# A Mamba layer on Trainium2: one bank of PSUM moved from the states of the scan to the small products beside it

## The chip, the cores and the metric

The kernel runs on one core of one Trainium2 chip. The core has a matmul engine (TensorE, "PE" in the profile, with its weight loads as "PEld"), a vector engine (VectorE, DVE), an activation engine (ScalarE, ACT), a general one (GpSimd, POOL) and a queue from which most DMAs are issued (SyncE, SP). Each engine works through its own instructions in order, and waits on semaphores for the others. Matmuls write into PSUM, which VectorE and ScalarE read and write too; in this kernel it is handed out in eight banks of 512 fp32 values a partition. The metric is the device time of one execution in microseconds, lower is better; times are medians of several executions.

## The reference

A network of four layers over an image of 2 x 256 x 48 x 48 in fp32: a Mamba layer (layer 0), linear attention with a convolution and a feed-forward (layer 1), attention and a graph-gated mixture (layer 2), sigmoid attention and a routed mixture (layer 3). The change lies in layer 0, whose core is a selective scan, run over the 2304 pixels once forward and once backward:

```python
def _selective_scan(u, delta, A, Bm, Cm, D):
    h0 = jnp.zeros((Bsz, d, A.shape[1]), u.dtype)
    def step(h, xs):
        d_t, B_t, C_t, u_t = xs
        dA = jnp.exp(d_t[..., None] * A)
        h = dA * h + (d_t * u_t)[..., None] * B_t[:, None, :]
        y = jnp.einsum('bdn,bn->bd', h, C_t)
        return (h, y)
    ...
    return ys.transpose(1, 0, 2) + u * D

def _mamba_branch(xi, z, conv_w, conv_b, xproj_w, dtproj_w, dtproj_b, A_log, D):
    ...                                     # depthwise convolution of 4 taps: xc
    xs = jax.nn.silu(xc + conv_b[None, :, None]).transpose(0, 2, 1)
    proj = xs @ xproj_w.T
    dt = jax.nn.softplus(proj[..., :DT_RANK] @ dtproj_w.T + dtproj_b)
    Bm = proj[..., DT_RANK:DT_RANK + D_STATE]
    Cm = proj[..., DT_RANK + D_STATE:]
    y = _selective_scan(xs, dt, -jnp.exp(A_log), Bm, Cm, D)
    return y * jax.nn.silu(z)

h = _layernorm(seq, ln_g, ln_b) + pos
xz = h @ in_proj_w.T
xi, z = (xz[..., :d_inner], xz[..., d_inner:])
y = (y_f + y_b) @ out_proj_w.T
out = seq + y
```

There are 512 inner channels (`DB` = 4 blocks of 128 partitions) and 16 states for each (`NS`). The scan is a recurrence along the pixels, one for each channel and state.

## The kernel before

Everything is fp32. Layer 0 cuts the 2304 pixels of each of the two images into six pieces of 384 (`W`). A piece in one direction of one image is a *scan*: 2 images x 2 directions x 6 pieces = 24 scans, in the list `order`. Each call of `scan` (L499) works through 4 blocks x 16 states = 64 states, and carries the last column of each over to the next piece in `state`.

For one state the engines pass a tile on:

- ScalarE writes the decay exp(dt * A) into a PSUM tile `hs` (L544). These tiles come from the pool `psh`, tag "hs": five banks before the change.
- VectorE runs the recurrence over it (L550 forward, L553 backward), with `db`, the product of dtu and B, which GpSimd makes for four states at a time (L527). For five of every eight states the result goes back into the same bank `hs`, for three into an SBUF tile `ho`.
- The result times C is the product `hc` (L558): made by VectorE from `hs`, by GpSimd from `ho`. Each of the two has four SBUF buffers.
- ScalarE copies the last column into `state` (L560), except in the last piece of a direction.
- TensorE adds `hc` to the output of its block by a matmul with the identity (L512), into `yp`. Those two banks (pool `psy`) stay as they are; L533 and L537 start them.

So a bank `hs` is held from the exponential until the product and the state copy have read it, or, where the result goes to `ho`, until the recurrence has.

Beside each scan runs other work, in small steps that are written into the loop after every second state (L568 to L572): `prepare` for the next scan, in 15 steps (convolution L311 and its copy L315, SiLU L321, the projection L327, the matmuls for dt L341 with L344 and L345, softplus L347 to L357, dtu on GpSimd L359); for the first ten scans `project_in` for a later piece, in 12 steps (layer norm L221 to L240, matmuls L247 and copies L252); after a backward scan `project_out`, in 2 steps (L368 and the sum L373), followed by the statistics of `piece_stats` (L138); and in the later scans the weights and contexts of layers 1 and 2 (`head_products`, `contexts`: pg, pu, pk, pc and others, L392 to L494). Each of these products takes one PSUM tile from the pool `ps`, tag "mm", through `hold` or directly: one bank before the change. It is free again when ScalarE or VectorE has read the product.

`hold` has a second case. Before the first scan (`scanning` is false) it takes its tiles from `psh`:

```python
    def hold():

        pool, tag = (ps, "mm") if scanning else (psh, "hs")
        return pool.tile([P, 512], F32, tag=tag, name="mm")[:, :W]
```

The order of instructions on each engine is made when the program is built, by the framework's ordering of what the source says, with the buffers that are free; it is not the order of the source line by line. ScalarE switches between tables for exponential, SiLU, logarithm and square root (ACT_TABLE_LOAD in the profile).

Of the kernel before, what the change touches and what calls it, by code (L numbers as in the profile page):

```python
# [24 lines left out]
PSUM = bass.MemoryType.PSUM  # L25
# [148 lines left out]
def layer0(ctx, E):  # L174
# [9 lines left out]
    nc, tc, p = E.nc, E.tc, E.p  # L184
# [5 lines left out]
    dr = ctx.enter_context(tc.tile_pool(name="l0d", bufs=2, space=DRAM))  # L190
    wp = ctx.enter_context(tc.tile_pool(name="l0w", bufs=2))
    up = ctx.enter_context(tc.tile_pool(name="l0u", bufs=1))
    psh = ctx.enter_context(tc.tile_pool(name="l0ps_h", bufs=5, space=PSUM))
    ps = ctx.enter_context(tc.tile_pool(name="l0ps_s", bufs=1, space=PSUM))
    psy = ctx.enter_context(tc.tile_pool(name="l0ps_y", bufs=1, space=PSUM))

    load_x(E, 0, 0)
# [1829 lines left out]
@with_exitstack  # L2027
def hybrid_kernel(ctx: ExitStack, tc: tile.TileContext, p: dict):
    E = Env(ctx, tc, p)
    layer0(E)  # L2030
    with tc.tile_pool(name="norm", bufs=1) as pool:

        E.xn = pool.tile([P, 2, T], F32, name="xn")
        with ExitStack() as kept:
            edges = Edges(kept, E)
            layer1(E, edges)
            with tc.tile_pool(name="gedge", bufs=1) as wp:
                edges.sort_rest(E, wp)
                layer2_attn(E)
            layer2_ffn(E, edges)  # L2040
        layer3(E)
    store_out(E)
# [73 lines left out]
```

## Time and profile before

| | |
|---|---|
| median of 3 runs | 5328.02 us (5325.92 to 5332.41) |
| profiled execution | 5324.93 us, span 5323.1 us |
| TensorE clock granted, mean | 0.963 |
| first and last recurrence of layer 0 | 101.9 and 2448.9 us |
| one scan, from its first recurrence to the next one's | 89 to 108 us, the last 80 us |
| one recurrence L550/L553 | 0.93 to 1.01 us |
| one product L558: VectorE, GpSimd | 0.54, 1.03 us |
| one exponential L544, one state copy L560 | 0.58, 0.15 to 0.19 us |
| one db L527 (four states) | 3.44 us |
| one ACT_TABLE_LOAD | 1.28 us, 65 of them before L544 |

The page gives for each engine its busy time over the whole program, and its share in 40 slices of 133 us. A row of instructions has the line, the engine, the tiles written and read, busy time and mean duration, then the idle time of the engine just before them and who ended it. A matmul of fp32 stands as two records, so four products of a convolution are "x8". A row of waits gives the waiting instruction, the one that ended the wait, the total, the count and the longest. In the timeline a line is the start, the duration, the engine, the line of the code and the tiles, with the idle time in brackets.

### The profile page before, as it was taken

Reading aid. Unit: us, or ns where it says so; the run is one execution under the profiler, and the core shown is the slowest. Engines: PE = TensorE matmul, PEld = TensorE weight load, DVE = VectorE, ACT = ScalarE, POOL = GpSimd, SP = SyncE. Lnnn points to the kernel's source line nnn. Section 1 sums busy time; section 2 is a strip of 40 time slices with the busy share of each in tenths; the row PEclk is TensorE's granted clock in tenths of the full one; section 3 lists DMA queues with packets and bytes.
Section 4 is the critical chain, followed back from the end, with each engine's and each line's share of the span. In section 5 each row is a group of like instructions: output and inputs, shape, how many; then the busy total and the mean of one; then the engine's idle time right before and its main releaser. Section 6 shows DMA issues by size and latency. Waiting matters only on the chain. (4 is left out here: it accounts for less than half of the span.)

```text
span 5323.1 us, 47473 instructions
## 1 busy us (share of the span) xinstructions
PE 4760.4 (89%) x15282; PEld 2640.7 (50%) x15282; DVE 3489.3 (66%) x5378; ACT 2385.4 (45%) x4985; POOL 2415.8 (45%) x1320
## 2 busy tenths in 40 slices
PE   7888888888888888888999989999999999999997
PEld 3444444444444444444555555556655555555675
DVE  4999898989898888899999344546734411212343
ACT  5767767765667667762223223432133322222221
POOL 2888887788888878884000000028712100000321
PEclk8999999999999999999999999999999999999998
DMA  4454454444444344443110000111121100000422
GB/s 154 169 174 170 164 178 165 168 177 166 163 165 161 137 157 161 149 152 118 38 48 28 3 16 0 35 32 31 19 96 48 48 6 6 7 9 9 85 82 95
DMA packets 187427, 504.63 MB, mean 95 GB/s; under 512 B 33591, under 2 KB 106683, under 8 KB 186908
## 3 DMA queue, kind: packets, MB, share of 16 engines
q1 hardware_dynamic: 178460, 488.74, 26.8%
q0 software_dynamic: 8704, 12.73, 1.6%
q8 instruction: 123, 2.02, 0.2%
q14 instruction: 140, 1.15, 0.1%
HBM read 425.88 MB, written 75.51 MB: 94 GB/s over the span
## 5 line engine op out<-in xcount | busy, mean ns | idle before, releaser
L512 PE MATMUL yp<-hc,ident 128*128 128x384 f32 x3072 | 1182.7, 516 | 205.6 <-DVE hc L558 165.2
L527 POOL TENSOR_TENSOR db<-dtu,bb 128x1536 f32<-128x1536 f32 x384 | 1322.4, 3444 | 53.1 <-DVE hs L553 13.5
L512 PEld LDWEIGHTS yp<-hc,ident 128*128 128x128 f32 x3072 | 571.6, 196 | 761.5 <-DVE hc L558 318.5
L558 POOL TENSOR_TENSOR hc<-ho,cc 128x384 f32<-128x384 f32 x576 | 587.4, 1027 | 236.6 <-DVE ho L553 106.0
L558 DVE TENSOR_TENSOR hc<-hs,cc 128x384 f32<-128x384 f32 x960 | 499.6, 538 | 78.5 <-PE yp L512 77.2
L544 ACT ACTIVATE hs<-dt,negab 128x384 f32<-128x384 f32 x768 | 435.2, 581 | 94.9 <-DVE hc L558 45.2
L544 ACT ACTIVATE hs<-dt,negaf 128x384 f32<-128x384 f32 x768 | 434.5, 581 | 67.3 <-DVE hc L558 32.6
L550 DVE TENSOR_TENSOR_SCAN hs<-hs,state,db 128x384 f32<-128x384 f32 x400 | 395.1, 1007 | 34.5 <-POOL db L527 21.5
L553 DVE TENSOR_TENSOR_SCAN hs<-hs,state,db 128x384 f32<-128x384 f32 x400 | 393.1, 1004 | 34.2 <-POOL db L527 16.2
L1921 POOL DMA_INDIRECT xe<-xt_d,token x48 | 47.4, 988 | 755.1 <-issue 715.6
L311 PE MATMUL mm<-xw,w_cv 128*128 128x384 f32 x768 | 285.8, 514 | 57.0 <-ACT xs L315 18.0
L1856 PE MATMUL po<-at,xtok 128*128 128x384 f32 x864 | 329.7, 506 | 7.7 <-ACT at L1854 7.5
L1847 PE MATMUL sp<-qT,xn 128*128 128x384 f32 x864 | 317.2, 486 | 0.0
L1854 ACT ACTIVATE at<-sp 128x384 f32<-128x384 f32 x216 | 104.6, 490 | 472.7 <-PE sp L1847 472.6
L1503 PE MATMUL ph<-xn,w 128*128 128x384 f32 x768 | 286.7, 516 | 18.0 <-ACT hid L1507 7.0
L1061 POOL PARTITION_ALL_REDUCE most<-most x1 | 0.4, 381 | 625.4 <-issue 625.4
L800 PE MATMUL pf<-t,wfc 128*128 128x384 f32 x768 | 255.0, 487 | 3.7 <-ACT hid L804 2.7
L819 PE MATMUL po<-hid,wfc 128*128 128x384 f32 x768 | 253.6, 486 | 0.0
L553 DVE TENSOR_TENSOR_SCAN ho<-hs,state,db 128x384 f32<-128x384 f32 x240 | 239.0, 996 | 13.8 <-ACT hs L544 13.6
L550 DVE TENSOR_TENSOR_SCAN ho<-hs,state,db 128x384 f32<-128x384 f32 x240 | 238.7, 995 | 8.7 <-ACT hs L544 8.7
L560 ACT COPY state<-hs 128x1 f32<-128x1 f32 x800 | 117.6, 155 | 274.3 <-DVE hc L558 271.6
L311 PEld LDWEIGHTS mm<-xw,w_cv 128*128 128x128 f32 x768 | 146.7, 197 | 188.4 <-ACT xs L315 31.4
(464 smaller groups left out, 7984.0 us busy)
## 6 DMA issues: line engine op xcount, KB each, us to landing
bb<-bcd SPq DMA_DIRECT2D x192, 768.0 KB, 4.2
cc<-bcd SPq DMA_DIRECT2D x192, 768.0 KB, 4.2
xw<-xi_d SPq DMA_DIRECT2D x24, 774.0 KB, 5.7
w<-in_m_w SPq DMA_DIRECT2D x16, 1024.0 KB, 5.8
y_d<-y SPq DMA_DIRECT2D x32, 384.0 KB, 2.3
ye<-y_d SPq DMA_DIRECT2D x32, 384.0 KB, 3.3
xi_d<-xz SPq DMA_DIRECT2D x48, 192.0 KB, 2.3
z_d<-xz SPq DMA_DIRECT2D x48, 192.0 KB, 3.0
```

The costliest lines, as they stand in the source:

```text
L311: nc.tensor.matmul(px, lhsT=w_cv[b, s][:, d * 4 + k, :], rhs=xw[:, d, o : o + W], start=k == 0, stop=k == 3,)
L512: nc.tensor.matmul(yp[d], lhsT=E.ident, rhs=hc, start=False, stop=summed[d] == NS)
L527: nc.gpsimd.tensor_tensor(db, bc(dtu[:, d, :], [P, GN, W], 1), bb, ALU.mult)
L544: nc.scalar.activation(hs, dt[:, d, :], AF.Exp, scale=nega[s][:, d * NS + n : d * NS + n + 1])
L550: nc.vector.tensor_tensor_scan(to, hs, db[:, j], init, ALU.mult, ALU.add)
L553: nc.vector.tensor_tensor_scan(to[:, ::-1], hs[:, ::-1], db[:, j, ::-1], init, ALU.mult, ALU.add)
L558: (nc.gpsimd if on_pool else nc.vector).tensor_tensor(hc, to, cc[:, j, :], ALU.mult)
L800: nc.tensor.matmul(pf, lhsT=wfc1[:, k, f * P : (f + 1) * P], rhs=t1[:, k, :], start=k == 0, stop=k == 1,)
L819: nc.tensor.matmul(po[m], lhsT=wfc2[:, f, m * P : (m + 1) * P], rhs=hid[:, i, :], start=f == 0, stop=f == 15,)
L1503: nc.tensor.matmul(ph, lhsT=w1[:, e, k, f * P : (f + 1) * P], rhs=xn[:, k, c * W : (c + 1) * W], start=k == 0, stop=k == 1,)
L1847: nc.tensor.matmul(sp, lhsT=xn[:, k, t0 + i * P : t0 + (i + 1) * P], rhs=qT[:, k, c * W : (c + 1) * W], start=k == 0, stop=k == 1,)
L1856: nc.tensor.matmul(po[m], lhsT=xtok[:, i, m * P : (m + 1) * P], rhs=at, start=i == 0, stop=i == MT - 1,)
```

## The change

Two numbers. The pool of the `hs` tiles gets four buffers in place of five, the pool of the "mm" tiles two in place of one. With the two of `psy` that makes eight banks before and after. No operation changes, in kind, size or number.

```diff
     up = ctx.enter_context(tc.tile_pool(name="l0u", bufs=1))
-    psh = ctx.enter_context(tc.tile_pool(name="l0ps_h", bufs=5, space=PSUM))
-    ps = ctx.enter_context(tc.tile_pool(name="l0ps_s", bufs=1, space=PSUM))
+    psh = ctx.enter_context(tc.tile_pool(name="l0ps_h", bufs=4, space=PSUM))
+    ps = ctx.enter_context(tc.tile_pool(name="l0ps_s", bufs=2, space=PSUM))
     psy = ctx.enter_context(tc.tile_pool(name="l0ps_y", bufs=1, space=PSUM))
```

## The prediction

> **What bounds the kernel now.** I read the page's slices first, to find the stage that the change touches, then one window over that stage, the waits of VectorE, TensorE and ScalarE in it, and last the timeline of one place where VectorE runs dry. In each line of waits: who waited, for whom, total us, times, longest.
>
> ```profile
> PE 4760.4 (89%) x15282; PEld 2640.7 (50%) x15282; DVE 3489.3 (66%) x5378; ACT 2385.4 (45%) x4985; POOL 2415.8 (45%) x1320
> ...
> DVE  4999898989898888899999344546734411212343
> ```
>
> ```profile
> 100.00:2450.00 2350.00, 1971.32 (x5468) 986.05 (x5469) 2093.55 (x2740) 1592.08 (x3669) 1960.06 (x983) 0.96 0.47 162
> ```
>
> A slice is 133 us; the nines of VectorE end at about 2450 us. That is the Mamba layer, the only place where the two pools are used. In the window (busy us of PE, weight loads, DVE, ACT, POOL; then granted clock, DMA share, GB/s) VectorE works 2093.55 of 2350 us, 89%. It is the bound: 256 us of idle are all that buffers can give or take on it. TensorE at 84% is close behind, so its delays matter when they reach VectorE.
>
> ```profile
> DVE hc L558 <- PE yp L512: 77.2, 73, 10.5
> DVE hs L550 <- POOL db L527: 36.3, 29, 6.8
> DVE dt L356 <- ACT state L560: 28.9, 16, 3.1
> DVE hs L550 <- ACT hs L544: 14.4, 21, 2.2
> DVE ho L553 <- ACT hs L544: 13.8, 13, 2.5
> ```
>
> ```profile
> PE yp L512 <- DVE hc L558: 165.2, 158, 8.8
> PE yp L512 <- POOL hc L558: 38.0, 26, 3.1
> PE mm L311 <- ACT xs L315: 16.6, 13, 3.1
> PE mm L311 <- DVE xres L373: 16.5, 9, 2.6
> PE mm L247 <- ACT xz L252: 15.1, 12, 3.6
> ```
>
> VectorE's idle has two makers. TensorE: the products hc cannot be written because four earlier ones still wait for their matmul, 77.2 us. ScalarE: exponentials (hs) come late, 45.0 us over the four scan rows (14.4 and 13.8 above, 9.5 and 7.3 further down the view), and softplus sums (L355, L356) wait for ScalarE, 49.1 us. POOL's db, 60.4 us, has no part in the change. TensorE in turn spends about 174 us before beside matmuls (all rows that do not write yp, summed), mostly until ScalarE or VectorE has read the single bank "mm".
>
> ```profile
> 1021.77 4.54 PE L311 MATMUL mm<-xw,w_cv 128*128 128x384 f32 x8 [1.96 <-ACT xs L315]
> ...
> 1026.35 0.58 ACT L315 ACTIVATE xs<-mm,vec 128x384 f32<-128x384 f32 x1 [1.17 <-PE mm L311]
> ...
> 1027.33 0.58 ACT L544 ACTIVATE hs<-dt,negab 128x384 f32<-128x384 f32 x1
> 1027.93 1.28 ACT L321 ACT_TABLE_LOAD   x1
> ...
> 1029.22 1.48 ACT L321 ACTIVATE xs<-xs 128x1536 f32<-128x1536 f32 x1
> 1029.41 1.46 DVE L558 TENSOR_TENSOR hc<-hs,cc 128x384 f32<-128x384 f32 x3
> ...
> 1030.98 1.28 ACT L544 ACT_TABLE_LOAD   x1
> 1032.28 0.58 ACT L544 ACTIVATE hs<-dt,negab 128x384 f32<-128x384 f32 x1
> 1032.95 1.02 DVE L553 TENSOR_TENSOR_SCAN hs<-hs,state,db 128x384 f32<-128x384 f32 x1 [2.09 <-issue]
> ```
>
> This place shows both sides. TensorE waits 1.96 us for the bank, and ScalarE then 1.17 us for TensorE: one bank makes two in-order engines take turns. Right after it ScalarE leaves for the SiLU: from the end of one exponential (1027.91) to the start of the next (1032.28) are 4.37 us, VectorE lives on what had been put by, and stands idle 2.09 us. What it lives on are the hs banks.
>
> **The change, part by part.** No instruction is added, removed or resized, no DMA and no queue; the price is all in waits and in the order that is laid down when the program is built (the trace shows engines running several exponentials ahead of earlier state copies, so the order follows free buffers, not the source alone).
>
> *Five hs banks to four.* Counted over the trace, exponential by exponential: 1069 of 1536 start while four banks are still held, that is, they take the fifth; and ScalarE waits 148.2 us for a bank (rows of L544 for hc and ho: 77.9, 41.6, 28.7). At the start of a scan, 0 exponentials are ready beyond its own in 275 cases, 1 in 269, 2 in 665, 3 or 4 in 327. In the even stretches four banks suffice: exponential 0.58, scan 0.99, product 0.54, state copy 0.15, some 2.3 us and a few signals for a turn, against four states at 1.21 us each on VectorE (scan 0.92 from start to start, and 5/8 of 0.46 for the product) = 4.8 us. So the steady loop costs nothing; its cover is 2 us or so.
>
> The cost falls where ScalarE is away. Two such gaps recur in each of about 23 scans: SiLU (L321, 4 to 5 us between exponentials) and softplus (L347 to L353, 8 to 11 us, or two pieces of 4 to 6). VectorE is idle 4 to 4.6 us in most softplus gaps; at SiLU it is idle in some 18 (2 to 3 us in most), and not in five early forward ones, which enter with four exponentials ahead. Where it is dry already, a state less in stock is a state later: 1.21 us. 23 x 1.21 + 18 x 1.21 = 50 us. The square-root gap (L230, nine times) stays at nothing: the reciprocal (2.54 us) and the products of L238 and L240 fill it; without that cover it would be 9 x 1.21 = 11 us. Bounds: from below 0, if the banks were held at these gaps only by products stuck behind TensorE; from above 104, if besides each of the 269 scans with one ready came 0.2 us late. I take 50.
>
> *One mm bank to two.* I set each VectorE wait on yp against TensorE's waits for the bank in the 12 us before it and take the smaller. Example: at 1048.81 and 1054.36 VectorE waits 0.69 and 2.02 us, TensorE had lost 1.15 + 0.44 + 0.32 = 1.91 in the burst before: 1.9 of 2.7 can come back. In other clusters (1325, 1832, 2136) TensorE had lost next to nothing, it only had too many matmuls at once: 0. The sum over all clusters is about 44 us. Not all of it returns: a convolution block of four matmuls is 2.6 us, two may now be run back to back ahead of yp matmuls, and the evacuations still queue on ScalarE behind exponentials. I take 26, six tenths. Bounds: the other side is a loss, if blocks pushed forward hold up yp more than the stalls did; 20 us, a quarter of the wait seen, is my estimate. The high end is all 77.2.
>
> A rule speaks for the change here. The row: TensorE's 174 us before beside matmuls, 77.2 us of VectorE behind yp. The Trainium skill, "Perfetto Trace Analysis", section Matmuls, says that independent matmul groups should rotate through different PSUM banks, so that the evacuation of one overlaps the next one's matmuls. Taken alone it would credit the change with up to the 77.2 us and charge nothing. But the hs banks are the same kind of store for the bounding engine, and the same page's Optimization Strategy says that consistent bubbles on that engine can mean too little PSUM for the next tile. By the first rule the sum is -77; by the rows it is +50 - 26. I go with the rows: all eight banks were in use already.
>
> *The rest.* Before the first scan the beside products draw on the hs pool too, four buffers for five: a copy (L252, 0.47 us) is shorter than the two matmuls that fill the next bank (1.45 us), so nothing; if not covered, a few copies, 2 us. The last scan (2368 to 2449 us, nothing prepared beside it) has 0.55 us of VectorE idle and should stay.
>
> Sum: +50 - 26 = +24 us. Against the profiled execution (5324.93 us, span 5323.1 and 1.8 around it) 5349; that run is 3.1 us under the median 5328.02, so the median would come out near 5352. I say 5350.
>
> **Rivals.**
> A, the forecast: the supply of exponentials decides, +24. For it: 70% of exponentials use the fifth bank, and dry places recur at the same two steps of every scan. Against: many gaps begin with only one exponential ahead though five banks exist; the others held finished scans waiting for their product.
>
> B, faster: the relief of TensorE decides. At 1022 to 1029 us products are delayed while TensorE works through a convolution block and 14 yp passes, and that is what fills the hs banks. If TensorE runs without its 7 us of bank stalls a scan (174/24), products go at once, banks come back sooner, and four serve as well as five did. Then the loss is 10 and the gain 44: -34, 5294. It decides from the point where SiLU and softplus gaps begin with two exponentials ready instead of one.
>
> C, no difference: the second bank is hardly used. The beside steps are spaced (a prepare step every 5 us or so of the scan), many depend on ScalarE's result anyway (L327 on the SiLU, L341 on pr), and the planned order had put yp matmuls into most holes. Gain 15, loss 15: 5328.
>
> **How the numbers follow.** A 0.55, B 0.31, C 0.14. A alone spans 5335 (loss 30, gain 23) to 5405 (the loss near its upper bound, 90, gain 13). The whole range, 5294 to 5405, takes in the middle of B and leaves out the ends of both cases, about 2 in 10. About 0.2%, 10.7 us, is what a measurement of this kernel can tell from no change: faster by more 0.31, within 0.14, slower by more 0.55.
>
> **What would show it.** Right: VectorE's waits for hs <- ACT rise from 45 to about 80 us and those at L355/L356 from 49 to 65, hc <- yp falls to about 50, scans with none ready beyond their own rise well over 275, TensorE's waits for mm fall under 90. The other stages keep their lengths to about 2 us. Wrong: hc <- yp falls below 35 with the ScalarE waits where they were (B); or mm waits on TensorE stay above 140 (C); or hc <- yp rises, and convolution blocks stand back to back in the timeline: then the new order of TensorE, not the exponentials, is the loss.

## The result: faster by a quarter of a per cent, against the forecast

| | before | after |
|---|---|---|
| median | 5328.02 us (11 runs, 5319.59 to 5332.41) | 5314.33 us (11 runs, 5309.17 to 5320.61) |
| ratio | | 0.9975, 95% interval 0.9966 to 0.9985 |
| profiled execution, span | 5324.93, 5323.1 us | 5312.88, 5311.1 us |
| first to last recurrence of layer 0 | 2347.0 us | 2332.7 us |
| VectorE idle in that stretch | 254.2 us | 229.2 us |
| VectorE at work in that stretch | 2092.7 us | 2103.5 us |
| all after that stretch | 2874.2 us | 2874.1 us |

The change saves 13.7 us, all of it in layer 0: VectorE is idle 25.0 us less and at work 10.7 us more. The page's lines for the engines and for VectorE's slices, as shown of before:

```profile
PE 4771.6 (90%) x15282; PEld 2645.6 (50%) x15282; DVE 3498.4 (66%) x5378; ACT 2391.6 (45%) x4987; POOL 2426.1 (46%) x1320
...
DVE  4999989998899888899999344546724411212343
```

The same window over the Mamba layer (now a little of layer 1 is in it, since the layer ends 12 us sooner):

```profile
100.00:2450.00 2350.00, 1986.06 (x5483) 993.67 (x5481) 2116.14 (x2775) 1601.45 (x3676) 1974.91 (x986) 0.96 0.47 163
```

VectorE's waits in the window:

```profile
DVE hs L550 <- POOL db L527: 37.4, 32, 6.8
DVE dt L356 <- ACT ln L352: 32.4, 13, 4.1
DVE hs L553 <- ACT hs L544: 30.6, 21, 3.5
DVE hc L558 <- PE yp L512: 29.8, 21, 9.6
DVE hs L553 <- POOL db L527: 29.6, 23, 2.9
DVE dt L356 <- ACT state L560: 17.3, 9, 3.3
DVE hs L550 <- ACT hs L544: 13.8, 16, 2.6
```

And TensorE's:

```profile
PE yp L512 <- DVE hc L558: 212.6, 207, 6.7
PE yp L512 <- POOL hc L558: 39.3, 29, 2.1
PE mm L341 <- ACT pr L331: 23.6, 9, 4.3
PE mm L247 <- ACT xz L252: 19.6, 11, 4.4
```

VectorE's largest wait, for TensorE, fell from 77.2 to 29.8 us. TensorE's waits before products into mm, all rows that do not write yp summed, fell from 174 to 85 us, and the convolution (L311), which led them, has almost left the list. What is now large, L341 behind pr, waits for data and not for a bank. TensorE waits longer for hc instead (165.2 to 212.6): it keeps up. Part was given back on ScalarE's side: the four rows hs or ho <- ACT hs grew from 45.0 to 65.0 us, and the sums L355 and L356 wait 57.2 us for ScalarE where they waited 49.1. The longer work is in the sums: L355 to L357 last 129.0 us together before, 141.6 after.

The SiLU gap that the prediction showed is still there, as one of later time shows:

```profile
1122.49 1.28 ACT L321 ACT_TABLE_LOAD   x1
...
1123.78 1.48 ACT L321 ACTIVATE xs<-xs 128x1536 f32<-128x1536 f32 x1
...
1125.69 1.28 ACT L544 ACT_TABLE_LOAD   x1
...
1126.98 0.58 ACT L544 ACTIVATE hs<-dt,negab 128x384 f32<-128x384 f32 x1
...
1127.60 1.02 DVE L553 TENSOR_TENSOR_SCAN ho<-hs,state,db 128x384 f32<-128x384 f32 x1 [2.24 <-ACT hs L544]
```

2.24 us of VectorE idle here, 2.09 in the place shown of before.

### The profile page after: what moved, and what is told of

It reads as the page before. It is cut to its first block, busy times and chain, and to the rows that moved or that the text cites. A ratio compares the mean times of both kernels' runs of the same rounds, so it can differ in the third digit from the quotient of the medians.

```text
span 5311.1 us, 47493 instructions
## 1 busy us (share of the span) xinstructions
PE 4771.6 (90%) x15282; PEld 2645.6 (50%) x15282; DVE 3498.4 (66%) x5378; ACT 2391.6 (45%) x4987; POOL 2426.1 (46%) x1320
## 5 line engine op out<-in xcount | busy, mean ns | idle before, releaser
L512 PE MATMUL yp<-hc,ident 128*128 128x384 f32 x3072 | 1207.1, 522 | 257.2 <-DVE hc L558 212.6
L527 POOL TENSOR_TENSOR db<-dtu,bb 128x1536 f32<-128x1536 f32 x384 | 1342.5, 3496 | 101.6 <-issue 88.7
L558 POOL TENSOR_TENSOR hc<-ho,cc 128x384 f32<-128x384 f32 x576 | 575.9, 1008 | 219.5 <-DVE ho L553 104.5
L558 DVE TENSOR_TENSOR hc<-hs,cc 128x384 f32<-128x384 f32 x960 | 498.0, 538 | 34.9 <-PE yp L512 29.8
L311 PE MATMUL mm<-xw,w_cv 128*128 128x384 f32 x768 | 276.9, 490 | 10.2 <-DVE xres L373 3.9
L1507 ACT ACTIVATE hid<-ph,vec 128x384 f32<-128x384 f32 x192 | 110.4, 580 | 293.2 <-PE ph L1503 259.6
```

The lines of the kernel that those rows point to most:

```text
L311: nc.tensor.matmul(px, lhsT=w_cv[b, s][:, d * 4 + k, :], rhs=xw[:, d, o : o + W], start=k == 0, stop=k == 3,)
L512: nc.tensor.matmul(yp[d], lhsT=E.ident, rhs=hc, start=False, stop=summed[d] == NS)
L527: nc.gpsimd.tensor_tensor(db, bc(dtu[:, d, :], [P, GN, W], 1), bb, ALU.mult)
L558: (nc.gpsimd if on_pool else nc.vector).tensor_tensor(hc, to, cc[:, j, :], ALU.mult)
```

## The experiments

Each ran at least five times beside the kernel before on the same chip. The chips differ: before takes 5375 to 5376 us on those of e1 to e12 and 5328 on that of e13 and e14. The stage does not: from first to last recurrence the changed kernel takes 2332.7 us in the run above and 2331.5 in e5, on another chip; what follows the stage takes 2874 and 2924. So ratios to before are compared, and lengths of the stage. The last column splits the stage of the profiled execution into VectorE's idle time and its work; VectorE has the same instructions in all five.

| hs, mm banks | kernel | ratio to before (95%) | stage = idle + work, us |
|---|---|---|---|
| 5, 1 | before | 1 | 2347.0 = 254.2 + 2092.7 |
| 4, 1 | e1 | 1.0076 (1.0063 to 1.0090) | 2381.3 = 268.2 + 2113.1 |
| 4, 2 | the change, e5 | 0.9979 (0.9970 to 0.9988) | 2331.5 = 227.9 + 2103.6 |
| 3, 2 | e2 | 1.0053 (1.0039 to 1.0067) | 2366.5 = 226.6 + 2139.9 |
| 3, 3 | e3 | 1.0019 (1.0011 to 1.0027) | 2349.2 = 210.6 + 2138.6 |

### One part of the change alone (e1, e5)

```diff
-    psh = ctx.enter_context(tc.tile_pool(name="l0ps_h", bufs=5, space=PSUM))
+    psh = ctx.enter_context(tc.tile_pool(name="l0ps_h", bufs=4, space=PSUM))
     ps = ctx.enter_context(tc.tile_pool(name="l0ps_s", bufs=1, space=PSUM))
```

> Four hs banks, one mm bank, one bank of PSUM unused: the loss alone, without the gain. Two separate terms (supply of exponentials some 28 us, TensorE's relief some 42 us): 28 us over the kernel before, about 5356, and VectorE's waits hs <- ACT near 65 us as in the changed kernel, hc <- yp still near 77. The banks are held by products stuck behind TensorE, so the two parts work together: without the second mm bank the missing hs bank hurts more, 50 us or more, 5378. My prediction's term: 50. The missing bank is free in itself: 5328 within 10.

Measured: 5415.09 us against 5375.3, 40 us slower; the stage 2381.3 us.

> The changed kernel itself, to have it on one chip with the others: 0.9975 of the kernel before, as measured, within 0.001. With 40 us for the fifth hs bank (run e1) the second mm bank then brings 53.

Measured: 5365.91 us against 5376.29, ratio 0.9979; the stage 2331.5 us. The two parts are of opposite sign, and both large: the fifth hs bank is worth 40 us, the second mm bank 50 us (5415 to 5366; 49.8 us in the stage). VectorE's waits in e1:

```profile
DVE hc L558 <- PE yp L512: 60.8, 51, 10.2
DVE dt L356 <- ACT ln L352: 44.5, 17, 4.6
DVE hs L550 <- POOL db L527: 34.3, 31, 6.8
DVE hs L553 <- ACT hs L544: 23.6, 22, 2.9
DVE hs L550 <- ACT hs L544: 22.4, 24, 2.2
```

Of the 34 us that e1's stage is longer than that of before, 14 are idle of VectorE (268.2 for 254.2) and 20 are work that lasts longer: 17 of these are in L355 to L357 (145.7 us for 129.0), above all in L355 (duration min/median/max in ns, before and in e1):

```profile
L355 DVE TENSOR_TENSOR ex<-ex,dtu x23: 1734/1757/2273, 158.6 to 2340.1; 128x1536 f32<-128x1536 f32 x23
```

```profile
L355 DVE TENSOR_TENSOR ex<-ex,dtu x23: 1732/1885/4703, 159.7 to 2371.0; 128x1536 f32<-128x1536 f32 x23
```

Which of them take long depends on what GpSimd does beside them. In these two traces, and in those of e2 and e5, each sum of L355 to L357 with next to no GpSimd product beside it (under 5% of its time) takes 1.73 to 1.76 us. In e1 seven of all 24 L355 run beside one for more than half of their time, and take 4.24 us on the mean; before, none did.

Of the 49.8 us that the second mm bank brings back, 40 are idle and 10 are work. Waiting for TensorE at hc gives 32 of the idle (60.8 to 28.7), the small sums behind TensorE (L399, L412, L414, L222, L473) 9.5, the sums behind ScalarE 6, scans behind state copies 10; the scans' wait for db takes 14 back.

### Further banks moved (e2, e3)

```diff
-    psh = ctx.enter_context(tc.tile_pool(name="l0ps_h", bufs=4, space=PSUM))
+    psh = ctx.enter_context(tc.tile_pool(name="l0ps_h", bufs=3, space=PSUM))
     ps = ctx.enter_context(tc.tile_pool(name="l0ps_s", bufs=2, space=PSUM))   # e3: bufs=3
```

> Three hs banks, two mm banks, one bank unused: one more hs bank taken from the changed kernel. Separate terms: the supply shrinks again and more steeply, since three banks cover only 3.6 us of VectorE's work: 40 to 60 us over the changed kernel, 5355 to 5375. Banks held by late products only: with TensorE relieved few are held, so 10 us, 5325.

Measured: 5401.42 us, ratio 1.0053, 0.0074 or 40 us over the changed kernel. The fourth hs bank is worth what the fifth is, but it is paid for in another way. Scans wait 121.3 us for exponentials in place of 64.9, the sums for ScalarE 20.0 in place of 57.1, and in all VectorE's idle does not grow (226.6 for 227.9). The stage is longer by work that lasts longer: L355 to L357 take 160.9 us for 141.7, and the products L238 and L240 of the layer norm 40.7 for 31.4.

> Three hs banks, three mm banks, all eight in use: against the run with three and two it shows what a third mm bank brings. TensorE's waits before beside matmuls in the changed kernel are 85 us, of which 24 are for pr (data, not a bank). Separate terms: at most 15 us under the run with three and two. If TensorE's relief is worth more than I think: 30 us under.

Measured: 5386.33 us, ratio 1.0019, 15 us under e2, in the stage 17 us, 16 of them idle. The third mm bank is worth a third of the second. So the banks' price is steady on the side of the states and falls on the other, and 4 and 2 is the best of the splits that were run.

### Exponentials written to SBUF (e4)

```diff
-                    hs = psh.tile([P, 512], F32, tag="hs", name="hs")[:, :W]
+                    if on_pool:
+                        hs = wp.tile([P, W], F32, tag="ho", name="ho", bufs=5)
+                    else:
+                        hs = psh.tile([P, 512], F32, tag="hs", name="hs")[:, :W]
...
-                    to = wp.tile([P, W], F32, tag="ho", name="ho", bufs=4) if on_pool else hs
+                    to = hs
```

> The changed kernel, and the exponentials of the three states of eight whose scan goes to ho are written into ho itself (in SBUF, five buffers for four; pr gets one buffer for two to make room), so that four banks serve five states of eight. Separate terms: the supply is better than with five banks, so the 20 to 28 us of ScalarE waits that the change brought go, and more of them: 5285 to 5295. Banks held by late products only: the changed kernel's 5314 within 8. A cost that neither has: a write to SBUF and a scan from SBUF may last longer than from PSUM (at most 0.1 us for 576 states, 58 us of ScalarE, which is not the bound, and as much of VectorE, which is).

Measured: 6012.53 us, ratio 1.1179, 637 us slower. It says nothing of the supply, for the scan itself changed. The recurrences into ho of before, whose decay is in PSUM (duration min/median/max, in ns):

```profile
L550 DVE TENSOR_TENSOR_SCAN ho<-hs,state,db x240: 982/991/1018, 192.1 to 1863.3; 128x384 f32<-128x384 f32 x120
```

and of e4, where the decay and db are both in SBUF:

```profile
L553 DVE TENSOR_TENSOR_SCAN ho<-ho,state,db x240: 984/1728/4180, 212.6 to 2357.4; 128x384 f32<-128x384 f32 x120
```

The shortest is as short as before, the median 0.74 us and the longest 3.2 us longer, about the length of a db on GpSimd (3.44 us). The page's rows give means of 1.90 and 1.98 us where before has 1.00, so 480 of the 576 such scans alone last some 450 us longer. The Trainium skill, "SBUF — State Buffer", section Who interferes with whom, says that a VectorE instruction with two SBUF inputs contends with a GpSimd instruction that reads SBUF. The durations agree with it. Of e4's 480 such scans, those with next to no GpSimd product beside them take 0.99 us on the mean and 1.02 at most; those with one beside them for over 90% of their time take 2.1 us on the mean and up to 4.17. My bound of 0.1 us a state looked at the write and the read alone.

### One pool for both (e6)

```diff
-    psh = ctx.enter_context(tc.tile_pool(name="l0ps_h", bufs=4, space=PSUM))
-    ps = ctx.enter_context(tc.tile_pool(name="l0ps_s", bufs=2, space=PSUM))
+    psh = ctx.enter_context(tc.tile_pool(name="l0ps_h", bufs=6, space=PSUM))
...
-        pool, tag = (ps, "mm") if scanning else (psh, "hs")
-        return pool.tile([P, 512], F32, tag=tag, name="mm")[:, :W]
+        return psh.tile([P, 512], F32, tag="hs", name="mm")[:, :W]
```

(pg, pu, pk and pc take theirs from `psh` too; code lines stand two lower than before.)

> The states and the beside products draw on one pool of six banks: whoever needs a bank next gets the next free one. If both terms are supply (each bank has its worth at its moment), this is better than either fixed split: 15 to 40 us under the changed kernel, ratio to before 0.990 to 0.995. If the ordering gives the banks to exponentials first and beside products come late, or exponentials are held up behind beside products: slower than the changed kernel, ratio 0.998 to 1.01.

Measured: 5615.19 us, ratio 1.0441. VectorE's waits, from 100 us to 2680:

```profile
DVE hs L548 <- ACT hs L542: 92.1, 55, 6.6
DVE hs L551 <- ACT hs L542: 90.2, 50, 4.9
DVE ho L548 <- ACT hs L542: 53.6, 45, 4.0
DVE xres L371 <- PE mm L366: 42.7, 20, 3.9
DVE ho L551 <- ACT hs L542: 36.7, 42, 2.2
```

Six shared banks starve the scans worse than three of their own do: 272.6 us behind exponentials, against 121.3 in e2. For a bank that the scan still holds, though, the exponentials wait less than before (L542 behind hc and ho: 94.6 us, before 148.2). ScalarE stands at other instructions of its order instead: at the products that it has to read (L313, L329, L342, L250) it waits 155.5 us for TensorE, where it waited 36.2. The order looks to be the loss, more than a lack of banks; why it came out like this stays open. Of the 244 us that the stage is longer than that of before, 135 are idle of VectorE and 109 are work that lasts longer.

### Without ScalarE's absences (e7, e8, e9)

```diff
-        nc.scalar.activation(xs, xs, AF.Silu)
-        if not fwd:
-            nc.scalar.activation(y, y, AF.Silu)
...
-            nc.scalar.activation(ex[:, d, :], pd, AF.Abs, bias=E.v(f"dt_b_{s}", d, 1))
...
-        nc.scalar.activation(ex, ex, AF.Exp, scale=-1.0)
-        nc.scalar.activation(dtu, ex, AF.Identity, bias=one[:, 0:1])
-        nc.scalar.activation(ln, dtu, AF.Ln)
-        nc.scalar.activation(dtu, dtu, AF.Identity, bias=one[:, 1:2])
-        nc.vector.tensor_tensor(ex, ex, dtu, ALU.subtract)
-        nc.vector.tensor_tensor(dt, dt, ln, ALU.add)
-        nc.vector.tensor_tensor(dt, dt, ex, ALU.add)
```

> The kernel before without ScalarE's two long absences: SiLU of x and of z, and everything of softplus but the relu (L344, L347 to L357), are left out, so their activations, their table loads and three sums on VectorE are missing; all else stays. By itself it shows what the absences cost: per scan some 13 us of ScalarE and 5.5 us of VectorE work and some 6 us of VectorE's idle go, so 23 x 11 = 250 us less, ratio 0.95. It is the reference for the next run.

Measured: 5204.86 us, ratio 0.9676 (0.9663 to 0.9689): 171 us less, where I expected 250. Part of the saving is hidden in this trace: eight of the layer norm's products L240 run beside a GpSimd product nearly from end to end and take 3.3 to 3.8 us, the others some 0.6 (one 1.3). The rows of e7 and of e8, the next kernel (min/median/max in ns):

```profile
L240 DVE SCALAR_TENSOR_TENSOR h<-h,vec,pos x20: 586/608/3785, 107.7 to 977.1; 128x384 f32<-128x384 f32 x20
```

```profile
L240 DVE SCALAR_TENSOR_TENSOR h<-h,vec,pos x20: 586/606/617, 108.6 to 947.3; 128x384 f32<-128x384 f32 x20
```

> The same (SiLU and softplus left out) with four hs banks in place of five, one mm bank. If the fifth bank is worth its 40 us because ScalarE is away twice a scan, which is how my prediction got its 50, it is worth little here: at most 10 us over the run before it. If the steady loop lacks the bank (or products stuck behind TensorE hold the banks), the loss stays: 30 to 45 us over it.

Measured: 5204.02 us, ratio 0.9679 (0.9666 to 0.9692). By the times the fifth hs bank, worth 40 us with the absences, is worth nothing without them. The traces show two differences that cancel: VectorE's idle is 7.4 us longer in e8 than in e7 (207.8 for 200.4), and its work 20.4 us shorter, since the L240 of e8 take 12.1 us in all and those of e7 37.7. So the steady loop loses little with four banks, 7 us of idle where e1 lost 14; that the fifth is worth nothing there is not shown. SiLU and softplus also took with them the sums L355 to L357, in which e1 lost 17 us.

> SiLU and softplus (but for the relu) left out as in runs e7 and e8, four hs banks, two mm banks: against e8 (ratio 0.968 to before) it is the second mm bank's worth where ScalarE has no long absence. With the absences it was 50 us (e1 against e5). If TensorE's own taking of turns makes it, it stays, 35 to 50 us under e8, ratio 0.958 to 0.961, and VectorE's hc <- yp falls from 49 to under 25. If it comes mostly from TensorE standing behind a bank that ScalarE doesn't read while it is away, it falls to under 15, ratio 0.965 to 0.968.

Measured: 5187.47 us, ratio 0.9645 (0.9632 to 0.9658), 0.0034 or some 18 us under e8. Most of the second mm bank's 50 us is gone as well: VectorE's idle falls by 11 us, where it fell by 40 from e1 to e5. The rows of e8 and e9 for VectorE behind TensorE:

```profile
DVE hc L545 <- PE yp L499: 49.3, 54, 9.5
```

```profile
DVE hc L545 <- PE yp L499: 33.0, 32, 9.6
```

It fell by 16 us and stayed above 25, where a large effect would have taken it; the measurement lies between the two numbers given, nearer the small one. The second mm bank, then, is worth most where SiLU and softplus run.

### Where the second bank is needed (e10)

```diff
-    ps = ctx.enter_context(tc.tile_pool(name="l0ps_s", bufs=2, space=PSUM))
+    ps = ctx.enter_context(tc.tile_pool(name="l0ps_s", bufs=1, space=PSUM))
...
-    def hold():
+    def hold(tag="mm"):
-        pool, tag = (ps, "mm") if scanning else (psh, "hs")
+        pool, tag = (ps, tag) if scanning else (psh, "hs")
...                                        # the three products of prepare:
-            px = hold()
+            px = hold("pp")
-        pj = hold()
+        pj = hold("pp")
-            pd = hold()
+            pd = hold("pp")
```

> Four hs banks, and the two mm banks dedicated: one to the products of prepare, one to all others (project_in, project_out, contexts and heads). If the relief comes from two kinds of beside work no longer sharing one bank: as the changed kernel, ratio 0.997 to 0.999. If it comes from consecutive products of one kind (four convolution blocks, eight products of project_in) following each other without waiting for the read: most of the 50 us is lost again, ratio 1.003 to 1.008.

Measured: 5352.75 us, ratio 0.9957 (0.9944 to 0.9971), against the changed kernel's 0.9979 (0.9970 to 0.9988): not slower, and by how much faster is not certain, since the intervals touch. Products of one kind must take turns again here, and TensorE waits for that; VectorE does not wait longer:

```profile
PE mm L247 <- ACT xz L252: 26.6, 13, 3.8
PE mm L311 <- ACT xs L315: 22.2, 11, 5.6
```

```profile
DVE hc L558 <- PE yp L512: 26.5, 18, 8.0
```

TensorE's waits before beside products are 111 us here, 170 in e1 and 86 in e5; VectorE's wait for it is as short as in e5 (28.7). What the second bank is needed for, then, is to part the two streams: a product of `prepare` no longer waits until one of the other work has been read, nor the other way round.

### Softplus in smaller steps (e11, e12, e13), and both together (e14)

```diff
         nc.scalar.activation(ex, ex, AF.Exp, scale=-1.0)
+        yield
...
         nc.scalar.activation(ln, dtu, AF.Ln)
+        yield
...
-            beside.append((prepare(nb, s2, c2, ready), 15, 25))
+            beside.append((prepare(nb, s2, c2, ready), 17, 25))
```

> The changed kernel with softplus in smaller steps: one more yield behind L347 and one behind L352, 17 steps for 15, so that exponentials can run between its long activations. If the absences set the price of an hs bank (e8), the 4 us of idle at softplus halve: 23 x 2 = 46 us at most, I expect 25 to 45 under the changed kernel, ratio 0.990 to 0.994. If the exponentials are held up by banks rather than by ScalarE's absence: the changed kernel's 0.998.

Measured: 5355.65 us, ratio 0.9962 (0.9948 to 0.9975), 0.0017 or 9 us under the changed kernel, less than expected, and the intervals overlap.

> The kernel before (five hs banks, one mm bank) with the same two yields. Shorter absences also make the fifth hs bank worth less, so the change should be worth more on top of the yields than the 10 to 14 us it is worth without them: this one at ratio 0.993 to 0.997, 15 to 40 us above the run e11. If the two do not meet: 10 to 14 us above it.

Measured: 5381.85 us, ratio 1.0014 (1.0005 to 1.0023). Alone, the yields slow the kernel before by 6 us; on top of them the change brings 26 us.

> Softplus in smaller steps (the two yields), four hs banks, one mm bank. If both terms scale with the length of the absences: the fifth hs bank is worth 15 to 30 us (this one that much above e12's ratio 1.0014, so 1.004 to 1.007) and the second mm bank 30 to 45 (e11 at 0.9962). If only the presence of an absence counts: 40 and 60, ratio 1.009.

Measured: 5359.15 us against 5328.45, ratio 1.0055 (1.0041 to 1.0069). With the yields the fifth hs bank is worth 22 us (1.0014 to 1.0055), about half, and the second mm bank 50 us (0.9962 to 1.0055), the same. But the half that is gone is not the idle: from e12 to e13 VectorE's idle grows by 21.7 us, more than the 14.0 of e1, and its work, which grew by 20.4 in e1, shrinks by 2.1. So no run shows that the price of either bank follows the length of the absences. The test is a weak one, since the gaps of more than 3.5 us between exponentials are no shorter in sum (531 us in e12, 504 before).

> Four hs banks, the two mm banks dedicated (prepare, all others) as in e10, and softplus in smaller steps as in e11. If the two gains add (12 us and 9 us under the changed kernel on the same chip): ratio 0.993 to 0.995. If both take the same idle: 0.9955 to 0.997.

Measured: 5301.64 us against 5328.45, ratio 0.9951 (0.9938 to 0.9965), the fastest of all. Its interval overlaps those of e10 and e11, so that the two gains add is not shown; that it is faster than before, by 27 us, and than the change, is.

## Why the prediction was wrong

**The second mm bank, "I take 26, six tenths": this is the step that failed.** It measured 50 us, in the place of 26, and above the 44 that the count gave before the discount. So the sum became +40 - 50 = -10, in the place of +50 - 26 = +24, and changed its sign. (The 50 is measured with four hs banks. With five, where the count was made, it can't be: that takes nine banks.) The discount of 18 was for convolution blocks run back to back ahead of yp. VectorE's wait on yp fell by 47 us from before to after, and by 32 from e1 to e5; with the discount I had 26. In e10, where the blocks can't run back to back, the kernel is some 12 us faster than the change, with intervals that touch; if that is what they cost, the gain without them is above 60 us, not 44. The count also took VectorE's waits on yp alone, while a second bank freed the sums that wait for TensorE directly (9.5 us) and scans behind state copies (10); ScalarE, which makes these copies, waits 24.2 us for L311 in e1 and 4.9 in e5. And it took the smaller of two waits at each place as if the order stayed; the order was made anew.

**The fifth hs bank, "I take 50": near in size, but mostly by luck.** e1 measured 40. The working priced idle alone, a state less in stock at 23 gaps of softplus and 18 of SiLU, and of idle e1 has only 14 us more. Counted from the end of one exponential to the end of the next, in gaps of more than 2.5 us, VectorE's idle at softplus went from 87.6 to 90.1 us, where 28 were priced, and at SiLU from 39.4 to 53.5, where 22 were priced. Of these 14, 9 fell in four of the five early forward scans, which I had left out since they enter with four exponentials ahead. Nor was the stock at these gaps smaller on the mean: those with SiLU, softplus's exponential or the logarithm begin with 1.56 exponentials ready on the mean before, and 1.64 in e1. The other 20 us are work that lasts longer, above all L355, which now runs beside GpSimd. This I had put at nothing, with "the price is all in waits" and with VectorE's 256 us of idle as all that buffers can give or take; e1, e2 and e6 took 20, 47 and 109 us more than before by longer work alone. (A smaller error: the count of 1069 exponentials on the fifth bank lets a bank go with its product. The state copy holds it too, and with it they are 1171 of 1536.)

**The two terms were set beside each other, and meet in the same place.** e9 finds 18 us for the second bank without SiLU and softplus, against 50 with. In the trace of before, 66 of the 77.2 us of VectorE behind yp fall within ScalarE's absences (the 72 gaps of more than 3.5 us between exponentials with over 3 us of ScalarE's work in them, 454 us of the stage), and the idle that e1 adds lies in the gaps of SiLU and softplus as well. This place in e1 shows how:

```profile
1067.38 1.48 ACT L347 ACTIVATE ex<-ex 128x1536 f32<-128x1536 f32 x1
1067.55 1.56 PE L247 MATMUL mm<-h,w_in 128*128 128x384 f32 x4
...
1068.94 2.10 PE L512 MATMUL yp<-hc,ident 128*128 128x384 f32 x6
1069.79 0.56 DVE L558 TENSOR_TENSOR hc<-hs,cc 128x384 f32<-128x384 f32 x1 [1.51 <-PE yp L512]
...
1070.91 1.28 ACT L352 ACT_TABLE_LOAD   x1
1070.95 1.56 PE L247 MATMUL mm<-h,w_in 128*128 128x384 f32 x4
1071.08 0.56 DVE L558 TENSOR_TENSOR hc<-hs,cc 128x384 f32<-128x384 f32 x1 [0.73 <-PE yp L512]
...
1073.72 1.76 DVE L356 TENSOR_TENSOR dt<-dt,ln 128x1536 f32<-128x1536 f32 x1 [2.09 <-ACT ln L352]
```

ScalarE is in softplus, no exponential comes, and all that VectorE has left are products hc, which wait for a TensorE that is behind with yp and takes products of `project_in` in between. I had read the yp waits and the dry places as two stores that could be priced one by one. How much a late TensorE lengthens an absence for VectorE is not measured.

**Rival B.** Its point of decision was that "SiLU and softplus gaps begin with two exponentials ready instead of one". Of such gaps of more than 3.5 us, 42 of 55 began with one before and 19 of 51 after. But in e1, where TensorE has no second bank, it is 24 of 51: most of the shift came with the order for four hs banks, not from TensorE's relief. B had the direction; its loss of 10 was too low (40) and its gain of 44 not far off (50).

**What the marks said.** The mm waits of TensorE under 90: they are 85. The other stages within 2 us: they are. hs <- ACT from 45 to about 80: 65. The sums from 49 to 65: 57. hc <- yp about 50: 29.8, below the 35 that was given for B, with ScalarE's waits not where they were but 28 us higher. Scans with no exponential ready beyond their own well over 275: 296; those with one went from 269 to 843, so the reserve did shrink by one and mostly did not run out. POOL's db, which was to have no part: from 60.4 to 67.0. "Before the first scan nothing": the first recurrence starts at 104.3 us in one profile of the changed kernel and at 102.0 in the other, for 101.9 before.

**The rule that was weighed.** The Trainium skill, "Perfetto Trace Analysis", section Matmuls, has independent groups rotate through banks. Here that brought 50 us for the second bank, and 15 for the third. The rule's full credit (77) is too high, and my cut of it to 26 was too deep. In e10 no stream rotates, each has one bank, and the gain is there all the same: here it was enough that the two streams do not share a bank.

## What to carry to other kernels

When a buffer is moved from one use to another, look first where each use runs short: if both do so in the same stretch (here, while ScalarE is away), separate counts of waits are a weak price for the two effects, and relief of the engine that is behind can be worth more than its own row (50 us here, 32 of them in it). Measure the halves by themselves, with one buffer left unused: 40 us lost and 50 us gained made a sum of 10, which a small error in either turns round. Then split each difference into idle time and longer work of the bounding engine before you say what the buffer did: e7 and e8 take the same time, and differ by 7 us in the one and 20 in the other. When several streams share a buffer, try one for each before giving all of them more: in e10 that was at least as good.

## What the runs showed of the hardware

A recurrence on VectorE into ho, with one input in PSUM and one in SBUF, takes 0.98 to 1.02 us in the trace of before, whether a GpSimd product runs beside it for over 90% of the time (0.99 on the mean) or next to none (1.00). With both inputs in SBUF (e4) it takes 0.99 us with next to none beside it, and 2.1 on the mean, up to 4.17, with one for over 90% of the time. The PSUM banks of the states are therefore worth more than their storage: they keep the bounding engine out of GpSimd's way.

The sums of softplus show the same, with both inputs in SBUF: L355 takes 1.75 us with next to no GpSimd product beside it and up to 4.70 with one. So does L240 in e7 (0.6 and 3.8). None of these instructions was changed. Other numbers of buffers gave another order, which moved them beside GpSimd or away from it; L355 to L357 alone became 13 us longer in the change, 17 in e1 and 32 in e2.
